# Layer 0 of a two-layer graph network: where a tile's projection and its two groups of transposes stand, and in which order its pieces are read out

## The chip, the cores and the metric

The kernel runs on one core of a Trainium2 chip. TensorE (PE) multiplies matrices and writes them to PSUM, which is divided into eight banks of 512 fp32 numbers a partition. ScalarE (ACT) and VectorE (DVE) read PSUM and the on-chip memory; GpSimd (POOL) works on the on-chip memory in this kernel; SyncE (SP) issues most of the loads. The metric is the device time of one execution in microseconds (us). Times are compared as medians of several runs; traces and profiles come from one profiled execution.

## The reference

A batch of 8 graphs shares one adjacency matrix `adj` (2048 x 2048, rows scaled to sum 1); each of the 2048 nodes has 64 features. Two layers are applied. Cut to what is computed:

```
x, adj: (8, 2048, 64), (2048, 2048)
# layer 0: three supports I, A, 2 A A - I; weights made per node from a 16-wide embedding
w   = einsum('nd,dkio->nkio', embedding, weight0)        # d = 16, k = 3, i = o = 64
b   = einsum('nd,do->no', embedding, bias0)
xg  = [x, A x, (2 A A - I) x]
out = einsum('bnki,nkio->bno', xg, w) + b
x   = layernorm(x + out)
# layer 1: [x, A x, (2 A A - I) x] twice over, times one weight (320 x 64), + bias1
x   = layernorm(x + out1)
```

Layer 0 costs most in the product with 16 weight matrices a support, which are then summed with the node's own 16 embedding numbers.

## The kernel before, in words

The kernel works in four stages. The first hop (A x, to 123 us) and the second hop (A A x, to 226 us) are large products with the adjacency matrix. Layer 0's own products run from 226 to 521 us, and layer 1 from there to the end.

**Layer 0** works on 16 tiles of 128 nodes, in the loop at the end of `pattern` (lines 897 to 939). For a tile three operands are prepared, the tile's features (`of_x`, from a load `xt`), their first hop (`of_hop`) and their second hop (`of_second`). Operand k is kept as three fp32r parts, high, low and a mixture, made by `parts` in three steps: a cast on ScalarE (L327, `hl`), a subtraction on VectorE (L329, `parts`), and a combination, which is one VectorE instruction where `quick` is set (L332), else one of ScalarE (L334) and one of GpSimd (L335). The first hop must be transposed first: eight TensorE transposes of 64 x 64 blocks (`transposed`, L315) into a PSUM tile `pt` of two banks.

`mix0` then runs eight **pieces**, one for each quarter u of the batch and half h of the 16 weight matrices. A piece's product (L423) is 18 matmuls of 64 rows x 512 columns into a PSUM tile `pm` of two banks; two such matmuls use the two halves of TensorE's rows, so they stand as nine pairs. A piece is read out in one of three ways:

- kind "D": one VectorE instruction multiplies the product by the embedding numbers into a tile `aside` (L439), and a VectorE reduction over the eight matrices follows later ("reduce", L468);
- kind "R": eight ScalarE instructions scale the product (L452), and the same VectorE reduction follows;
- kind "P": eight ScalarE instructions scale it, and GpSimd sums ("sum", three instructions of L457, then "add", L461).

GpSimd adds the reduced parts to the tile's sum ("add_reduced", L472). The tile is then scaled to unit variance in four steps spread over the next tile (`scaled_to_unit`: n1 = squares on ScalarE, L368; n2 = a VectorE sum, L379; root on ScalarE, L382; n3 = VectorE's reciprocal, L384, and six GpSimd instructions, L385 to L390).

A tile t whose features are finished is transposed in turn (`transpose`: eight more transposes of L315 into another `pt`, then a ScalarE copy to `hT`, L321), and `project` multiplies it with layer 1's weights (L493, eight fp32 matmuls of 192 columns into two PSUM tiles `pu`); six ScalarE copies (L502) bring the results back. That happens while the next tile is in work.

**What sets the order.** Every instruction of ScalarE, VectorE and GpSimd in this stage goes through `ordered`, which keeps each engine's instructions in the order in which the program writes them. TensorE's instructions and the loads' places follow from that order and from what is ready, as the framework lists them. What is written between which pieces stands in the lists `at[0]` to `at[8]`: `at[n]` is written before piece n, so behind piece n - 1. PSUM tiles come from one pool of four pairs of banks (`bank`), handed out in turn: a new tile waits until the readers of the tile four places earlier are done. Operands' parts, `aside` tiles, `hT` and `sums` come from small pools handed out likewise.

In before, a tile t from 1 to 14 has this order on TensorE: the first product, the hop's transposes for tile t + 1, products two to seven, the feature transposes of tile t - 1, the eighth product, the projection of tile t - 1. The last tile has an order of its own, in which layer 1's first operands (`early`) are prepared as well.

Of the kernel before, what the change touches and what calls it, by code (L numbers as in the profile page):

```python
# [9 lines left out]
F32 = mybir.dt.float32  # L10
# [8 lines left out]
P = 128  # L19
B, N, C = 8, 2048, 64  # L20
NT = N // P
D = 16
# [19 lines left out]
def pattern(  # L42
# [22 lines left out]
    nc = tc.nc  # L65

    def pool(stack, name, bufs, **kw):
        return stack.enter_context(tc.tile_pool(name=name, bufs=bufs, **kw))
# [3 lines left out]
    xcpool = pool(ctx, "fxc", 4)  # L72
# [13 lines left out]
    def bank(name):  # L86

        return psum.tile([P, 2, 512], F32, tag="ps", name=name)
# [9 lines left out]
    def bc(s, t):  # L98
        return z[s][t].rearrange("p (b c) -> p b c", c=C)
# [8 lines left out]
    root = work.tile([P, B], F32, tag="ln_s", name="root")[:, :1]  # L108
    part = keep.tile([P, B], F32, tag="part", name="part")
# [19 lines left out]
    def ordered(ins):  # L129
        if in_order:  # L130
            tc.keep_in_program_order(ins)
# [47 lines left out]
    def weights():  # L179

        vec = nc.vector

        w24 = const.tile([P, C], F32, tag="w24", name="w24")
        yield vec.tensor_add(w24, wl[:, 2, :], wl[:, 4, :])
        yield vec.tensor_sub(v[:, 0, :], wl[:, 0, :], w24)
        for h in range(2):
            q = slice(h * C, (h + 1) * C)
            yield vec.tensor_add(v[q, 0, :], v[q, 0, :], ident[q, q])
        yield vec.tensor_add(v[:, 1, :], wl[:, 1, :], wl[:, 3, :])
        yield vec.tensor_scalar_mul(v[:, 2, :], w24, 2.0)  # L190


        mean = means[:, :4]
        yield vec.tensor_reduce(mean[:, :3], v, AX.X, ALU.add)
        yield vec.tensor_reduce(mean[:, 3:], bias1, AX.X, ALU.add)
        yield vec.tensor_scalar_mul(mean, mean, 1.0 / C)
        yield vec.tensor_tensor(v, v, mean[:, :3].unsqueeze(2).to_broadcast([P, 3, C]), ALU.subtract)
        yield vec.tensor_tensor(bias1, bias1, mean[:, 3:].to_broadcast([P, C]), ALU.subtract)
# [10 lines left out]
    def weight_parts():  # L209
        vec = nc.vector  # L210
        yield vec.tensor_sub(w[0], w[0], w[2])
        yield vec.tensor_scalar_mul(w[2], w[2], 2.0)
        yield from centre(w[0], 8)
        yield from centre(w[2], 8 + 2 * D)
        for k in (0, 2, 1):
            if k == 1:
                yield from centre(w[k], 8 + D)
                yield vec.tensor_scalar_mul(emb_sb, emb_sb, 1.0 - 1.0 / SPLIT)
            yield nc.scalar.copy(w_high[k], w[k])
            yield vec.tensor_tensor(w_low[k], w[k], w_high[k], ALU.subtract)  # L220
            yield vec.scalar_tensor_tensor(w[k], w_low[k], SPLIT, w_high[k], ALU.mult, ALU.add)
            yield vec.tensor_scalar_mul(w_mixed[k], w[k], SPLIT / (SPLIT - 1.0))
            yield vec.tensor_scalar_mul(w_low[k], w_low[k], -SPLIT)
# [82 lines left out]
    def by_half(tt):  # L306
        return tt.rearrange("p j (h n) -> p h j n", h=2)

    def transposed(src, pt=None):

        pt = bank("pt") if pt is None else pt
        for j in range(B // 2):
            for h in range(2):
                q = slice(h * C, (h + 1) * C)
                nc.tensor.transpose(pt[:, h, j * C : (j + 1) * C], src[q, 2 * j * C : 2 * (j + 1) * C], ident[q, q])  # L315
        return pt[:, :, : B // 2 * C].rearrange("p h (j n) -> p h j n", n=C)

    def transpose(src, tag, pt=None):

        tt = xcpool.tile([P, B // 2, P], F32, tag="ln_xc", name=tag)  # L320
        ordered(nc.scalar.copy(by_half(tt), transposed(src, pt)))  # L321
        return tt

    def parts(src, to, view, quick=False):

# [80 lines left out]
    def begin_sum(t):  # L406
        ordered(nc.gpsimd.tensor_tensor(bc(0, t), bc(0, t), ebias[:, t : t + 1, :].to_broadcast([P, B, C]), ALU.add))
# [77 lines left out]
    def project(t, hT, pus=None):  # L485


        for g in range(2):
            pm = bank("pu") if pus is None else pus[g]
            for i in range(2):  # L490
                for j in range(2):
                    q = slice(j * C, (j + 1) * C)
                    nc.tensor.matmul(  # L493
                        pm[:, j, i * 3 * C : (i + 1) * 3 * C], lhsT=hT[q, 2 * g + i, :], rhs=v[q],
                        start=True, stop=True,
                    )
            got = pm[:, :, : 6 * C].rearrange("p j (i k c) -> p j i k c", i=2, k=3)

            order = ["p (i j) c -> p j i c", "p (j i) c -> p j i c", "p (j i) c -> p j i c"]
            to = [bc(k, t)[:, 4 * g : 4 * g + 4, :].rearrange(order[k], j=2) for k in range(3)]  # L500
            for k in range(3):
                ordered(nc.scalar.copy(to[k], got[:, :, :, 2 - k, :]))  # L502
# [249 lines left out]
    pieces = chain(weights(), weight_parts())  # L752
# [74 lines left out]
    last_h = {}  # L827
    sums3 = []

    def last_transposed():  # L830
        last_h["T"] = transpose(h, "hT", sums3[1][0])

    def last_projected():
        project(NT - 1, last_h["T"], (sums3[1][1], sums3[1][0]))
# [46 lines left out]
    def early(i, *kinds):  # L881

        got = third_got.setdefault(i, {})
        for lead, part in sorted(third[i], key=lambda part: -part[0]):
            if part.__name__ in kinds:
                part(got)
        third[i] = [part for part in third[i] if part[1].__name__ not in kinds]

    def go(it):
        return lambda: next(it)  # L890

    s = ("load_sum", "operands")
    h, norm = None, None
    tt = first_tile[0]
    coming = operands(1)
    everything = range(B // 2)
    for t in range(NT):
        got, last = {}, t == NT - 1
        at = [[] for _ in range(9)]
        n1, n2, root, n3 = [lambda: next(norm)] * 4 if t else [nothing] * 4  # L900

        if not last:
            following, of_x, of_hop, of_second = coming
            of_hop = of_hop()
            at[1] += [go(of_x)] * (1 if t else 3)
            at[1] += [n1, lambda: begin_sum(t + 1)]
            if t + 2 < NT:
                at[1] += [lambda: times_r(t + 2)]
            at[1] += [go(of_hop)]
            at[2] += [("reduce", 0, 1), n2, go(of_hop), go(of_hop), ("reduce", 2, 0)]  # L910
            at[3] += [root]
            at[4] += [n3, go(of_second), ("reduce", 3, 0)]
            if t + 2 < NT:
                at[4] += [lambda: got.update(coming=operands(t + 2))]
            at[5] += [("reduce", 1, 1), go(of_second), go(of_second), ("add_reduced", 0, (2, 3))]
            at[7] += [("reduce", 2, 1), ("sum", 0)]
            at[7] += [lambda: got.update(hT=transpose(h, "hT"))] if t else []
            at[8] += [("add", 0, (0, 1)), ("reduce", 3, 1), ("add_reduced", 1, everything)]
            pieces = [(2, 0, "R"), (0, 1, "D"), (3, 0, "R"), (0, 0, "P"), (1, 1, "D"), (1, 0, "P"), (2, 1, "D"), (3, 1, "D")]
        else:  # L920
            at[1] += [n1, n2, root]
            at[2] += [n3, lambda: early(0, "y_high", *s), lambda: early(1, "load_sum")]
            at[3] += [("reduce", 0, 1), ("sum", 0), lambda: early(0, "y_low")]
            at[4] += [lambda: early(1, "y_high", "operands")]
            at[5] += [("reduce", 1, 1), ("reduce", 2, 0), lambda: early(1, "y_low"), ("add", 0, (0, 1))]
            at[6] += [lambda: got.update(hT=transpose(h, "hT")), lambda: early(2, "y_high")]
            at[7] += [("reduce", 2, 1), ("reduce", 3, 0), ("add_reduced", 0, (2, 3)), lambda: early(3, "y_high")]
            at[8] += [("reduce", 3, 1), ("add_reduced", 1, everything), lambda: early(2, "y_low"), lambda: early(3, "y_low")]
            pieces = [(0, 0, "P"), (1, 0, "P"), (0, 1, "D"), (2, 0, "R"), (1, 1, "D"), (3, 0, "R"), (2, 1, "D"), (3, 1, "D")]
        norm_now = mix0(t, tt, at, pieces)  # L930
        if t:
            project(t - 1, got["hT"])
        if "coming" in got:
            coming = got["coming"]
            next(coming[1])
            next(coming[1])
        norm, h = norm_now, z[0][t]
        if not last:
            tt = following
# [481 lines left out]
```

## Time and profile before

| What | Value |
|---|---|
| Time, median of 3 runs (lowest to highest) | 757.3 us (756.75 to 757.43) |
| The profiled execution's own time, and its span in the trace | 756.74 us, 755.0 us |
| Busy over the span: PE, DVE, ACT, POOL | 744.3, 618.1, 453.4, 277.9 us |
| Layer 0, 226.5 to 521 us (294.5): PE, DVE, ACT, POOL | 293.1, 271.7, 218.6, 208.7 us |
| Two tiles in the middle, 283.5 to 320.2 us (36.7): PE, DVE, ACT, POOL | 36.7, 34.1, 27.6, 27.6 us |
| Granted TensorE clock, share of full speed | 0.997 |

How to read it: "busy" is the time in which an engine has an instruction under way. Matmuls overlap and their ends are modelled, so what counts on TensorE is the time from one start to the next, and whether a row says that it was idle and for whom it waited. The chain that ended last is followed back from the last instruction; an engine with a high share of that chain sets the time. A row of a timeline gives start, length, engine, line, operation, output <- input, and in brackets the idle time ahead of it with the instruction that ended it.

### The profile page before, as it was taken

How to read it: one execution, taken by the hardware profiler on the slowest of the kernel's cores; microseconds unless marked ns; L12 is line 12 of the kernel's file. 1: busy time of each engine (PE TensorE's matmuls, PEld its weight loads, DVE VectorE, ACT ScalarE, POOL GpSimd, SP SyncE). 2: the span in 40 equal slices, each digit the busy share in tenths (PEclk: the TensorE clock that was granted, in tenths of full speed). 3: DMA queues.
4: the chain of work that ended last, by engine and by line, in shares of the span. 5: the costliest groups of instructions: out<-in, count | busy, mean ns of one | idle time of the engine just before them, and what ended most of it. 6: DMA issues, size and time to landing. Idle time of an engine off the chain costs nothing.

```text
span 755.0 us, 13518 instructions
## 1 busy us (share of the span) xinstructions
PE 744.3 (99%) x4942; PEld 613.0 (81%) x4942; DVE 618.1 (82%) x965; ACT 453.4 (60%) x1106; POOL 277.9 (37%) x299
## 2 busy tenths in 40 slices
PE   9999999999999999999999999999999999999995
PEld 6887888888888788888888888887788888888885
DVE  6768888999978999999999999979588557778563
ACT  5437444878755777777777777778877662112111
POOL 0001111133253877777777777664000000021430
PEclk9999999999999999999999999999999999999998
DMA  9998987555420000000000000004454454665621
GB/s 322 376 400 282 326 279 278 175 160 168 153 85 15 16 16 16 15 15 17 20 24 15 16 15 1 2 30 127 128 165 142 137 171 138 180 183 167 205 88 47
DMA packets 73691, 96.49 MB, mean 128 GB/s; under 512 B 5009, under 2 KB 48529, under 8 KB 73489
## 3 DMA queue, kind: packets, MB, share of 16 engines
q1 hardware_dynamic: 62208, 76.66, 32.2%
q10 hardware_dynamic: 11408, 18.89, 6.8%
q8 instruction: 41, 0.67, 0.4%
q14 instruction: 34, 0.27, 0.1%
HBM read 76.65 MB, written 18.87 MB: 127 GB/s over the span
## 4 chain that ended last, share of the span: by engine, by line
PE 92%; DVE 5%; issue 1%; POOL 1%; ACT 0%; DVEq 0%; POOLq 0%
PE pm L423 29%; PE accT L697 27%; PE acc L269 15%; PE a L269 10%; PE accT L269 6%; PE pu L493 2%; DVE aside L439 2%; DVE sums L468 1%; PE pt L315 1%; DVE parts L332 1%; PE first L145 1%; PE accT L853 1%; DVE parts L329 1%; ACT aside L452 0%; PE accT L493 0%
## 5 line engine op out<-in xcount | busy, mean ns | idle before, releaser
L697 PE MATMUL accT<-s,hl 128*128 128x512 f32 x896 | 206.1, 391 | 0.4 <-DVE aside L439 0.4
L697 PEld LDWEIGHTS accT<-s,hl 128*128 128x128 f32 x896 | 167.4, 188 | 36.7 <-DVE aside L439 0.9
L452 ACT ACTIVATE aside<-pm,pack_sb 128x128 f32<-128x128 f32 x512 | 140.2, 402 | 40.2 <-PE pm L423 40.2
L423 PE MATMUL pm<-wh,hl 64*128 64x512 f32 x768 | 154.6, 399 | 0.7 <-DVE aside L439 0.7
L423 PE MATMUL pm<-wm,parts 64*128 64x512 f32 x768 | 150.1, 388 | 0.0
L423 PE MATMUL pm<-wl,parts 64*128 64x512 f32 x768 | 149.7, 387 | 0.0
L684 ACT CAST s<-raw 128x1024 fp32r<-128x1024 bf16 x104 | 110.1, 1059 | 37.0 <-ACT hl L249 27.6
L468 DVE TENSOR_REDUCE sums<-aside 128x128 f32<-128x1024 f32 x96 | 115.9, 1210 | 3.2
L269 PE MATMUL acc<-hl,s 128*128 128x512 f32 x512 | 116.9, 390 | 0.0
L269 PEld LDWEIGHTS acc<-hl,s 128*128 128x128 f32 x512 | 95.9, 188 | 20.8 <-DVE z L578 0.9
L249 ACT CAST hl<-z 128x256 fp32r<-128x256 f32 (+1 forms) x96 | 47.8, 516 | 62.8 <-PE acc L269 21.6
L439 DVE TENSOR_TENSOR aside<-pm,pack_sb 128x1024 f32<-128x1024 f32 x64 | 78.3, 1223 | 8.7 <-PE pm L423 6.3
L423 PEld LDWEIGHTS pm<-wm,parts 64*128 64x128 f32 x768 | 71.9, 184 | 15.7
L423 PEld LDWEIGHTS pm<-wh,hl 64*128 64x128 f32 x768 | 72.3, 185 | 15.0 <-DVE aside L439 1.0
L457 POOL TENSOR_TENSOR aside<-aside 128x1024 f32<-128x1024 f32 (+2 forms) x48 | 71.6, 1491 | 32.3 <-ACT aside L452 29.8
L423 PEld LDWEIGHTS pm<-wl,parts 64*128 64x128 f32 x768 | 72.1, 185 | 13.8
L269 PE MATMUL a<-hl,s 128*128 128x512 f32 (+1 forms) x352 | 73.4, 370 | 0.0
L253 DVE TENSOR_TENSOR hl<-z,hl 128x512 fp32r<-128x512 f32 (+1 forms) x96 | 57.8, 610 | 16.6 <-ACT hl L249 7.6
L269 PEld LDWEIGHTS a<-hl,s 128*128 128x128 f32 x352 | 61.9, 188 | 11.3
L403 POOL TENSOR_TENSOR s<-s,part 128x8 f32<-128x8 f32 x16 | 7.0, 440 | 166.9 <-DVE s L402 145.8
L302 POOL TENSOR_TENSOR z<-z,got 128x512 f32<-128x512 f32 x3 | 4.8, 1622 | 144.1 <-ACT got L301 144.1
L368 ACT ACTIVATE sq<-z 128x512 f32<-128x512 f32 x31 | 20.0, 651 | 48.8 <-DVE z L304 46.6
(138 smaller groups left out, 948.4 us busy)
## 6 DMA issues: line engine op xcount, KB each, us to landing
raw<-in_adj SPq DMA_DIRECT2D x58, 512.0 KB, 6.0
raw<-sums_of SPq DMA_DIRECT2D x64, 256.0 KB, 2.9
sums_of<-z ACTq DMA_DIRECT2D x16, 512.0 KB, 6.8
raw<-quarters SPq DMA_DIRECT2D x32, 256.0 KB, 2.7
raw<-in_adj SPq DMA_DIRECT2D x16, 384.0 KB, 3.5
quarters<-seen ACTq DMA_DIRECT2D x16, 256.0 KB, 5.9
xt<-in_xT SPq DMA_DIRECT2D x16, 256.0 KB, 2.7
z<-in_x SPq DMA_DIRECT2D x15, 256.0 KB, 6.7
```

The source lines that it names most:

```text
L249: ordered(nc.scalar.copy(to[0], src))
L253: ordered(nc.vector.tensor_tensor(to[1], src, to[0], ALU.subtract))
L269: nc.tensor.matmul(accs[i], lhsT=s[:, i * P : (i + 1) * P], rhs=hl[h], start=(first and h == 0), stop=(last and h == 1),)
L368: ordered(nc.scalar.activation(sq, src, AF.Square))
L423: nc.tensor.matmul(pm[:, j], lhsT=tt[k][n][q, u, :], rhs=w_parts[n][k][q, ds, :], start=(k == 0 and n == 0), stop=(k == 2 and n == 2),)
L439: ordered(nc.vector.tensor_tensor(side_by_side(a), got, e, ALU.mult))
L452: ordered(nc.scalar.activation(to[d], got, AF.Copy, scale=emb_sb[:, t, h * DD + d : h * DD + d + 1]))
L457: ordered(nc.gpsimd.tensor_tensor(to, to, more, ALU.add))
L468: ordered(nc.vector.tensor_reduce(to, src, AX.X, ALU.add))
L493: nc.tensor.matmul(pm[:, j, i * 3 * C : (i + 1) * 3 * C], lhsT=hT[q, 2 * g + i, :], rhs=v[q], start=True, stop=True,)
L684: ordered(nc.scalar.copy(s, got["raw"]))
L697: nc.tensor.matmul(acc[i][:, c], lhsT=hl[h][:, i * P : (i + 1) * P], rhs=S[:, c * 512 : (c + 1) * 512], start=(kk == 0 and h == 0), stop=( ...
```

## The change

The change touches only layer 0's loop and splits `transpose` in two, so that the ScalarE copy (`keep_transposed`) can be written apart from the transposes.

- For tiles 0 to 14 the hop's transposes for the next tile but one, and the feature transposes of the tile before, are written between two tiles, behind the projection, and go into the two halves of one PSUM tile `pt` (columns 0 to 255 and 256 to 511 of each of its two banks). ScalarE's cast of the hop half is written there too. The copy of the feature half (`hT`) is written behind the next tile's first piece.
- So a projection comes one tile later: behind tile t stands the projection of tile t - 2. The last tile takes the projection that is left behind its second piece, and its own feature transposes and projection as before.
- The pieces of tiles 0 to 14 go R, D, P, D, P, D, R, D instead of R, D, R, P, D, P, D, D.
- The third operand's steps start one place earlier, and GpSimd's "sum" and "add" stand in `at[6]` behind them; the reductions and additions of the quarter 3 move to the end of the tile. In the last tile, the preparation of layer 1's third operand moves ahead of the two last reductions.

```diff
-    def transpose(src, tag, pt=None):
-
-        tt = xcpool.tile([P, B // 2, P], F32, tag="ln_xc", name=tag)
-        ordered(nc.scalar.copy(by_half(tt), transposed(src, pt)))
+    def keep_transposed(got):
+        tt = xcpool.tile([P, B // 2, P], F32, tag="ln_xc", name="hT")
+        ordered(nc.scalar.copy(by_half(tt), got))
         return tt
+
+    def transpose(src, pt=None):
+        return keep_transposed(transposed(src, pt))
...
+        if t > 1:
+            at[1] += [lambda: hT.append(keep_transposed(hT.pop()))]
         if not last:
             following, of_x, of_hop, of_second = coming
-            of_hop = of_hop()
-            at[1] += [go(of_x)] * (1 if t else 3)
-            at[1] += [n1, lambda: begin_sum(t + 1)]
+            if t == 0:
+                of_hop = of_hop()
+                at[1] += [go(of_hop), go(of_x), go(of_x)]
+            at[1] += [go(of_hop), go(of_x), n1, lambda: begin_sum(t + 1)]
             if t + 2 < NT:
                 at[1] += [lambda: times_r(t + 2)]
-            at[1] += [go(of_hop)]
-            at[2] += [("reduce", 0, 1), n2, go(of_hop), go(of_hop), ("reduce", 2, 0)]
-            at[3] += [root]
-            at[4] += [n3, go(of_second), ("reduce", 3, 0)]
+            at[2] += [("reduce", 0, 1), go(of_hop), n2, ("reduce", 2, 0)]
+            at[3] += [root, go(of_second)]
+            at[4] += [n3, ("reduce", 1, 1), go(of_second), go(of_second)]
             if t + 2 < NT:
                 at[4] += [lambda: got.update(coming=operands(t + 2))]
-            at[5] += [("reduce", 1, 1), go(of_second), go(of_second), ("add_reduced", 0, (2, 3))]
-            at[7] += [("reduce", 2, 1), ("sum", 0)]
-            at[7] += [lambda: got.update(hT=transpose(h, "hT"))] if t else []
-            at[8] += [("add", 0, (0, 1)), ("reduce", 3, 1), ("add_reduced", 1, everything)]
-            pieces = [(2, 0, "R"), (0, 1, "D"), (3, 0, "R"), (0, 0, "P"), (1, 1, "D"), (1, 0, "P"), (2, 1, "D"), (3, 1, "D")]
+            at[6] += [("reduce", 2, 1), ("sum", 0), ("add", 0, (0, 1))]
+            at[8] += [("reduce", 3, 0), ("reduce", 3, 1), ("add_reduced", 0, (2, 3)), ("add_reduced", 1, everything)]
+            pieces = [(2, 0, "R"), (0, 1, "D"), (0, 0, "P"), (1, 1, "D"), (1, 0, "P"), (2, 1, "D"), (3, 0, "R"), (3, 1, "D")]
         else:
             at[1] += [n1, n2, root]
-            at[2] += [n3, lambda: early(0, "y_high", *s), lambda: early(1, "load_sum")]
+            at[2] += [lambda: project(t - 2, hT.pop()), n3, lambda: early(0, "y_high", *s), lambda: early(1, "load_sum")]
...
-            at[6] += [lambda: got.update(hT=transpose(h, "hT")), lambda: early(2, "y_high")]
-            at[7] += [("reduce", 2, 1), ("reduce", 3, 0), ("add_reduced", 0, (2, 3)), lambda: early(3, "y_high")]
-            at[8] += [("reduce", 3, 1), ("add_reduced", 1, everything), lambda: early(2, "y_low"), lambda: early(3, "y_low")]
+            at[6] += [lambda: hT.append(transpose(h)), lambda: early(2, "y_high")]
+            at[7] += [("reduce", 2, 1), lambda: early(3, "y_high")]
+            at[8] += [
+                lambda: early(2, "y_low"), ("reduce", 3, 0), ("add_reduced", 0, (2, 3)),
+                ("reduce", 3, 1), ("add_reduced", 1, everything), lambda: early(3, "y_low"),
+            ]
...
         norm_now = mix0(t, tt, at, pieces)
-        if t:
-            project(t - 1, got["hT"])
-        if "coming" in got:
-            coming = got["coming"]
-            next(coming[1])
-            next(coming[1])
+        if last:
+            project(t - 1, hT.pop())
+        else:
+
+            if hT:
+                project(t - 2, hT.pop())
+            pt = bank("pt")
+            if "coming" in got:
+                coming = [*got["coming"]]
+                coming[2] = coming[2](pt[:, :, : N // 8])
+                for part in (coming[1], coming[2], coming[1]):
+                    next(part)
+            if t:
+                hT.append(transposed(h, pt[:, :, N // 8 :]))
```

More of the change, by code (lines that the diff above doesn't have):

```diff
@@ L830, in last_transposed @@
     def last_transposed():
-        last_h["T"] = transpose(h, "hT", sums3[1][0])
+        last_h["T"] = transpose(h, sums3[1][0])
     def last_projected():
@@ L895, in pattern @@
     coming = operands(1)
-    everything = range(B // 2)
+    everything, hT = range(B // 2), []
     for t in range(NT):
```

## The prediction

> **What bounds the kernel now.** I read the chain that ended last first, because it says which engine a shorter or longer layer 0 would move; then TensorE's rows in order of time, for the price of each break; then ScalarE's and VectorE's rows, for what becomes ready when. From the page, and from the chain in order of time (start, length, what):
>
> ```profile
> span 755.0 us, 13518 instructions
> PE 92%; DVE 5%; issue 1%; POOL 1%; ACT 0%; DVEq 0%; POOLq 0%
> ```
>
> ```profile
> 301.91 0.24 PE pt L315 x8
> 302.15 12.33 PE pm L423 x108
> 314.48 0.25 PE pt L315 x8
> 314.73 2.12 PE pm L423 x18
> 316.85 1.30 PE pu L493 x16
> 318.15 2.06 PE pm L423 x18
> 320.22 0.25 PE pt L315 x8
> ```
>
> TensorE is the whole chain. A tile of layer 0 takes 18.33 us (projections start at 280.03 and 500.03, twelve tiles apart), of which 72 pairs of matmuls at 0.227 are 16.3; the rest is three breaks. TensorE's rows price them:
>
> ```profile
> 301.75 0.40 PE L315 MATMUL pt<-ident,z 64*128 64x64 f32 x8
> 301.96 0.48 PE L423 MATMUL pm<-wh,hl 64*128 64x512 f32 x2
> 302.28 0.39 PE L423 MATMUL pm<-wl,parts 64*128 64x512 f32 x2
> 302.51 0.39 PE L423 MATMUL pm<-wm,parts 64*128 64x512 f32 x2
> ...
> 316.46 0.39 PE L423 MATMUL pm<-wm,parts 64*128 64x512 f32 x2
> 316.69 1.46 PE L493 MATMUL pu<-v,hT 64*128 64x192 f32 x16
> 317.86 0.53 PE L423 MATMUL pm<-wh,hl 64*128 64x512 f32 x2
> 318.22 0.40 PE L423 MATMUL pm<-wl,parts 64*128 64x512 f32 x2
> ```
>
> Eight transposes cost 0.21 and a projection 1.17, start to next start. The first pair after a break takes 0.32 to 0.36 instead of 0.23. So all that putting the three breaks together can save is two restarts, some 0.2 us a tile. Between 266 and 520 no row of TensorE waits for anybody: there is nothing else to win there, and much that could start to wait.
>
> **The change, part by part** (line numbers of before; those behind L315 move by 2 in the changed file).
>
> *The transposes do not come together.* In the built order of the changed kernel, from tile 2 to 13, the projection and the eight hop transposes stand between two tiles, but the eight feature transposes stand inside the next tile's first product, behind 7 of its 18 matmuls, between the two halves of one pair. The build makes them wait for ScalarE's cast of the hop half (hl<-pt, L327), since both halves now lie in one tile of two banks. Before, the two groups had a bank pair each and the feature transposes waited for nothing late. When is that cast done? ScalarE now has to copy the projection out first, then cast the next x, then the hop. Its rows:
>
> ```profile
> 317.61 1.76 ACT L502 COPY z<-pu 128x256 f32<-128x256 f32 x6 [2.25 <-PE pu L493]
> 319.20 0.67 ACT L327 CAST hl<-xt 128x512 fp32r<-128x512 f32 x1
> ```
>
> ```profile
> 230.86 0.67 ACT L327 CAST hl<-xt 128x512 fp32r<-128x512 f32 x1
> 231.37 0.65 ACT L327 CAST hl<-pt 128x512 fp32r<-128x512 f32 x1
> ```
>
> Counted from the projection's start (316.69): copies begin at +0.92 (they wait for its first half), the x cast 1.59 later, the hop cast 0.51 later, and it lasts 0.65: +3.67. TensorE restarts 0.05 after what it waits for (a VectorE row ends at 520.97, TensorE starts at 521.02): **+3.72**. When could TensorE take the transposes? 1.17 + 0.21 is +1.38. Then the next tile's first product needs its bank pair. Four pairs go round; in between lie two for the projection and one for the transposes, so it is that of the last product, which VectorE must have read. The last product's matmuls end 0.16 after the projection's start, VectorE's read lasts 1.23: +1.5 at the earliest, +2.5 if VectorE is behind (below). Seven matmuls take 0.33 + 3 x 0.23 = 1.0. So TensorE is ready at +2.5 to +3.5 and waits 0.2 to 1.2 us, every time until +3.72.
>
> Behind the wait: 0.21 of transposes, 0.10 restart, and 137 matmuls. Their halves are now out of step (row half 1 has 69 left, half 0 has 68), so 69 slots at 0.227, 15.66. Sum 3.72 + 0.21 + 0.10 + 15.66 = **19.7 us a tile instead of 18.33, +1.37**. The wait itself is shown by no row of before. From below it costs nothing (cast early enough): 1.17 + 0.42 + the bank wait 0.1 + one restart 0.1 + 16.3 = 18.1; from above VectorE decides (20.4, next). I take 19.7, since every term of it has a row.
>
> *A rule to weigh.* No row of before has two engines at one bank pair at once. "PSUM — Partial Sum Buffer" of the Trainium skill, section "Terms", says that two engines at the same bank and quadrant at once is a collision error, reads against reads included; by that the two groups cannot overlap however the list is ordered, and the sum stands. If halves of a bank were independent, the transposes could go at once and a tile would take some 18.4.
>
> *VectorE.* Its read of the hop half (L329, 0.68) now waits for ScalarE's copy of the features, which stands behind the next tile's first piece: product's end 1.84 behind the transposes, 2.02 of evictions, 0.59 of copy. Everything else of VectorE's tile is queued behind that read. From there to its last product's read is, by start-to-start spacings of its rows, 0.72 + 0.61 (L329, L332), 4 x 1.23 (L439), 4 x 1.13 (L468), 0.59 (L379), 0.11, 0.72 + 0.61: 12.8. Closing the ring: 1.84 + 2.65 + 12.8 + 0.05 + 1.0 = 18.4, under 19.7, so it is not the bound; its last read ends about +2.5. But L332 can lose to GpSimd:
>
> ```profile
> 258.31 4.90 POOL L457 TENSOR_TENSOR aside<-aside 128x1024 f32<-128x1024 f32 x3 [0.69 <-ACT aside L452]
> 258.38 2.88 DVE L332 SCALAR_TENSOR_TENSOR parts<-hl,parts 128x512 fp32r<-128x512 f32 x1
> ```
>
> That took 2.88 instead of 0.69; beside GpSimd's shorter sums it takes 1.67 (302.39). One such loss a tile gives 19.4, two 20.4.
>
> *The third operand ahead of GpSimd's sum* removes the 2.88 of tile 1 and nothing in the later tiles, where its L332 already takes 0.69 (331.88). *Pieces in turn*: cost nothing either way, for the four bank pairs cover two ScalarE pieces in a row today (324.69 to 329, TensorE never waits). The load of the next x keeps its step and its place on SP's queue; no DMA is added or moved past another. Begin of the sum and the scaling by r stay in GpSimd's order.
>
> *Start.* Before, the second projection starts at 280.03. After: tile 0 ends at 243.25 as now; 0.21 hop transposes, 0.1, 16.4 of tile 1: 260.0; the first product of tile 2 starts at 260.2, seven matmuls to 261.2; the hop cast, behind no copies yet, ends at 261.36; then 0.21 + 0.10 + 15.66: 277.3. That is where the first projection starts, a tile later than now: **-2.7**, being the projection (1.3) that now goes to the last tile, and VectorE's waits of tile 1 and 2 (0.72 and 0.25, with restarts).
>
> *End.* Tile 15 takes the projection that is left (1.3) between its second and third product. It waits for a feature copy behind ScalarE's first piece (0.59 + 2.02 + the product: 0.9 of wait), and the fourth product for an eviction behind that (0.3). Its first product starts 2.5 behind the last projection instead of 1.17 (1.3). **+3.8**. Layer 1's wait of 0.41 at 521.02 and its restart go, as VectorE has one reduce less before its last read: -0.65.
>
> *Sum*: -2.7 + 12 x 1.37 + 3.8 - 0.65 = **+16.8**. The profiled execution took 756.74 (1.74 around its span of 755.0), 0.56 under the median of 757.3. So 773.5.
>
> **Rivals.**
> 1. *The cast gates (above)*: 773.5, with tiles of 19.45 to 20.0: 770 to 777. For it: the wait is in the built program and every length has a row.
> 2. *VectorE becomes the bound* through two losses to GpSimd a tile, 20.4: 12 x 0.7 more, 782. For it: the 2.88 row. Against: GpSimd's long sum now comes later.
> 3. *A cheaper gate*: the split pair costs no slot (0.23) and VectorE is early, or the cast comes 0.4 earlier: tiles of 19.1: 766.
> 4. *Faster*: the wait is covered. If the cast is done by +2.5, before TensorE has done its seven matmuls, tiles take 18.1: 12 x -0.23, -2.7, -0.65, and +2.5 at the end: 753. It decides at a cast end of +2.5; ScalarE's six copies alone end at +2.68, which speaks against it.
> 5. *It cancels out*: tiles of 18.4 and the dearer last tile: 758.
>
> **How the numbers follow.** Chances: 0.72, 0.10, 0.12, 0.04, 0.02. Range 765 to 780: rival 1 whole, rival 3, the near part of rival 2. A difference under 0.2% (1.5 us) can hardly be told from none here: faster 0.04, same 0.02, slower 0.94.
>
> **What would show it.** Right: twelve waits of TensorE ahead of the feature transposes (L315) released by ScalarE's hl cast; projections 19.7 apart; VectorE idle until ScalarE's feature copy; the waits at 262 and 521 gone. Wrong: projections 18.1 to 18.4 apart, or a TensorE that waits for VectorE longer than for ScalarE.

## The result and the profile after

The changed kernel takes 775.58 us (median; 775.49 to 775.81), the kernel before 757.02 beside it (756.62 to 757.43): ratio 1.0246, 95% interval [1.0228, 1.0263]. The profiled execution's span is 773.7 us, 18.7 more than before's 755.0. The granted clock is 0.998 (before: 0.997).

The page of the changed kernel, in the order in which before was read: span, shares of the chain that ended last, and the group of first matmuls (its last columns: idle time of TensorE ahead of it, and for whom).

```profile
span 773.7 us, 13482 instructions
...
PE 62%; DVE 17%; POOL 7%; ACT 7%; issue 6%; DVEq 0%; POOLq 0%
...
L425 PE MATMUL pm<-wh,hl 64*128 64x512 f32 x768 | 223.8, 394 | 9.8 <-DVE aside L441 9.8
```

TensorE had 92% of the chain and has 62%; in layer 0 the chain now runs through VectorE, ScalarE and GpSimd. TensorE has no more to do than before, so its rows around one gap between tiles tell what it stands for (start, length, and in brackets the idle time with the one that ended it):

```profile
338.53 0.32 PE L495 MATMUL pu<-v,hT 64*128 64x192 f32 x1
338.55 0.39 PE L425 MATMUL pm<-wm,parts 64*128 64x512 f32 x1
338.69 1.38 PE L495 MATMUL pu<-v,hT 64*128 64x192 f32 x14
339.62 1.75 ACT L504 COPY z<-pu 128x256 f32<-128x256 f32 x6 [0.51 <-PE pu L495]
...
341.02 0.50 PE L425 MATMUL pm<-wh,hl 64*128 64x512 f32 x2 [0.55 <-DVE aside L441]
341.20 0.68 ACT L329 CAST hl<-xt 128x512 fp32r<-128x512 f32 x1
...
341.73 0.64 ACT L329 CAST hl<-pt 128x512 fp32r<-128x512 f32 x1
...
341.83 0.39 PE L425 MATMUL pm<-wh,hl 64*128 64x512 f32 x1
...
342.47 0.46 PE L315 MATMUL pt<-ident,z 64*128 64x64 f32 x8 [0.26 <-issue]
342.71 0.47 PE L425 MATMUL pm<-wl,parts 64*128 64x512 f32 x1
342.75 0.47 PE L425 MATMUL pm<-wh,hl 64*128 64x512 f32 x1
```

There are two waits in a gap. The next tile's product starts at 341.02, when VectorE has read the product four pairs back (the forecast's "+2.5": it is +2.49). Seven matmuls later TensorE stops until 342.47, 0.10 after ScalarE's cast of the hop half has ended (341.73 + 0.64 = 342.37). The trace lists this second wait under "issue" or under a GpSimd instruction, but it ends 0.09 to 0.14 behind the end of the cast in all eleven gaps from 302 to 501; in kernel 2 below, where the same wait is longer, the list names the cast itself four times. Projections start at 279.03 and 516.35, twelve tiles apart: **19.78 us a tile**, where it was 18.33. (The first of the twelve takes 20.18: there TensorE waits 1.42 for VectorE, at 282.43, and the cast has long ended.)

VectorE's waits in the changed kernel (total, times, longest), and its chain in time through the middle of a tile (start, length, what):

```profile
DVE parts L331 <- ACT hT L320: 39.4, 12, 3.4
```

```profile
344.47 2.18 ACT aside L454 x8
346.65 0.48 ACT hT L320
347.12 0.02 issue
347.15 0.69 DVE parts L331
347.84 0.60 DVE parts L334
```

Twelve times VectorE stands 3.3 us until ScalarE has copied the features, behind the next tile's first piece. The wait is new, and the chain runs through it.

### The profile page after: what moved, and what is told of

It reads as the page before. It is cut to its first block, busy times and chain, and to the rows that moved or that the text cites. A ratio compares the mean times of both kernels' runs of the same rounds, so it can differ in the third digit from the quotient of the medians.

```text
span 773.7 us, 13482 instructions
## 1 busy us (share of the span) xinstructions
PE 751.4 (97%) x4942; PEld 642.1 (83%) x4942; DVE 607.0 (78%) x965; ACT 453.1 (59%) x1106; POOL 285.4 (37%) x299
## 4 chain that ended last, share of the span: by engine, by line
PE 62%; DVE 17%; POOL 7%; ACT 7%; issue 6%; DVEq 0%; POOLq 0%
PE accT L699 27%; PE acc L269 15%; PE a L269 9%; DVE sums L470 6%; DVE aside L441 6%; PE accT L269 6%; POOL aside L459 5%; ACT aside L454 4%; PE pm L425 3%; DVE parts L334 2%; DVE parts L331 2%; ACT hl L329 2%; POOL z L392 1%; ACT hT L320 1%; PE first L145 1%
## 5 line engine op out<-in xcount | busy, mean ns | idle before, releaser
L425 PE MATMUL pm<-wh,hl 64*128 64x512 f32 x768 | 223.8, 394 | 9.8 <-DVE aside L441 9.8
L425 PE MATMUL pm<-wl,parts 64*128 64x512 f32 x768 | 219.9, 388 | 0.0
L425 PE MATMUL pm<-wm,parts 64*128 64x512 f32 x768 | 219.2, 387 | 0.0
L425 PEld LDWEIGHTS pm<-wh,hl 64*128 64x128 f32 x768 | 120.7, 184 | 18.9 <-DVE aside L441 11.8
L425 PEld LDWEIGHTS pm<-wm,parts 64*128 64x128 f32 x768 | 120.5, 184 | 6.7
L425 PEld LDWEIGHTS pm<-wl,parts 64*128 64x128 f32 x768 | 120.1, 184 | 5.8
L459 POOL TENSOR_TENSOR aside<-aside 128x1024 f32<-128x1024 f32 (+2 forms) x48 | 77.6, 1617 | 7.0 <-ACT aside L454 4.5
L253 DVE TENSOR_TENSOR hl<-z,hl 128x512 fp32r<-128x512 f32 (+1 forms) x96 | 56.0, 591 | 16.0 <-ACT hl L249 7.2
```

The costliest lines, as they stand in the source:

```text
L253: ordered(nc.vector.tensor_tensor(to[1], src, to[0], ALU.subtract))
L425: nc.tensor.matmul(pm[:, j], lhsT=tt[k][n][q, u, :], rhs=w_parts[n][k][q, ds, :], start=(k == 0 and n == 0), stop=(k == 2 and n == 2),)
L459: ordered(nc.gpsimd.tensor_tensor(to, to, more, ALU.add))
```

## The experiments

All times are medians, with the kernel before timed on the same chip (756.9 to 757.1). A gate is a wait that every tile has to pass; a ring is the work from one such wait to the same wait of the next tile, and the longest ring sets the time of a tile. Theory A: the cast alone gates the tile. Theory B: VectorE's ring (its late read of the hop half and all that is queued behind it) lies close behind the cast and holds the tile once the cast does not. Theory C: the order of the pieces and additions uses VectorE up.

**1. Feature transposes ahead of the hop's cast.**

```diff
+            if t:
+                hT.append(transposed(h, pt[:, :, N // 8 :]))
             if "coming" in got:
...
-            if t:
-                hT.append(transposed(h, pt[:, :, N // 8 :]))
```

> The changed kernel, but the feature transposes are written ahead of the hop transposes and ScalarE's cast of the hop half; then TensorE does not wait for the cast, and the built order has projection and both groups together. The ScalarE copy of the features stays behind the next tile's first piece. Theory A (the cast alone sets the 19.8 us of a tile): the tile falls to 18.2 to 18.3 and the time to 757, twelve times 1.5 less. Theory B (VectorE's ring, held by its read of the hop half behind the feature copy, lies close behind): in the changed kernel it closes from one last read to the next in 19.7 us, of which 1.1 are the wait, the transposes and the broken pair in the first product; without them 18.6, so 12 x 1.2 less: 761. Theory C (neither; the new order of pieces and additions costs the time): 775.

Measured: 769.03, ratio 1.0155 [1.0138, 1.0171]; tiles of 19.33. All three numbers missed, A's by 12 us, B's by 8, C's by 6. TensorE's gap in this kernel:

```profile
337.19 1.46 PE L495 MATMUL pu<-v,hT 64*128 64x192 f32 x16
...
338.49 0.66 PE L315 MATMUL pt<-ident,z 64*128 64x64 f32 x16
...
340.06 0.49 PE L425 MATMUL pm<-wh,hl 64*128 64x512 f32 x2 [0.91 <-DVE aside L441]
```

The sixteen transposes stand together and no matmul waits for a cast; TensorE waits 0.9 a tile for VectorE instead. So A alone falls; whether C does, kernel 3 tells. VectorE's ring here is 19.3, not the forecast 18.4, and its two L334 of a tile show why: they took 1.26 and 1.42 beside GpSimd, where the forecast had an undisturbed one (0.69 long) for both. From the hop half's read (345.18) to the end of the last product's read (359.32) it takes 14.14, forecast 12.8; the two L334 are 1.30 of that.

**2. The copy of hT ahead of the first piece (the cast's gate stays).**

```diff
-            at[1] += [lambda: hT.append(keep_transposed(hT.pop()))]
+            at[0] += [lambda: hT.append(keep_transposed(hT.pop()))]
```

> The changed kernel, but the ScalarE copy of the features is written ahead of the next tile's first piece instead of behind it, so that VectorE's read of the hop half can come some 2 us earlier; the feature transposes still wait for the cast. Theory A: VectorE's waits go (39 us of idle time ahead of that read fall under 15), TensorE's waits of 0.55 for VectorE go, its waits for the cast grow by the same: time as the changed kernel, 775 within 1.5. Theory B in its strong form (VectorE's ring sets the time): 765 to 770. Theory C: 775, but with VectorE late as before.

Measured: 775.11, ratio 1.0243 [1.0226, 1.026]; tiles of 19.72, as theory A had it (VectorE's idle time ahead of that read falls from 39.4 to 6.1). TensorE's wait moves whole from VectorE to the cast:

```profile
341.59 0.46 PE L315 MATMUL pt<-ident,z 64*128 64x64 f32 x8 [1.03 <-POOL z L474]
...
361.36 0.46 PE L315 MATMUL pt<-ident,z 64*128 64x64 f32 x8 [1.07 <-ACT hl L329]
```

The cast ends at 341.49 and at 361.22, so it is the same wait under two names.

**3. Both edits.**

> Both edits: features transposed first, and copied ahead of the first piece. Theories A and B alike: neither wait is left; a tile is 1.17 of projection, 0.42 of transposes, one restart, and 16.3 of products, 18.1 to 18.2, and the time 755, with 754 to 757 as bounds. Theory C: 770 or more, since order of pieces and of the additions stays.

Measured: 756.07, ratio 0.9987 [0.9978, 0.9997], inside the bounds of A and B; tiles of 18.19 from 297 on. Its gap:

```profile
333.95 1.46 PE L495 MATMUL pu<-v,hT 64*128 64x192 f32 x16
...
335.25 0.66 PE L315 MATMUL pt<-ident,z 64*128 64x64 f32 x16
...
335.72 0.47 PE L425 MATMUL pm<-wh,hl 64*128 64x512 f32 x2
336.03 0.39 PE L425 MATMUL pm<-wl,parts 64*128 64x512 f32 x2
```

From 297 on no wait is left between tiles. The new order of the pieces is all in here, so C falls. The four kernels make a square: with both gates 775.6, without the cast's 769.0, without the copy's 775.1, with neither 756.1. Taking away one leaves the other ring, of 19.72 or 19.33, in charge.

**4. Hop cast ahead of the x cast.**

```diff
-                for part in (coming[1], coming[2], coming[1]):
+                for part in (coming[2], coming[1], coming[1]):
```

> The changed kernel, but ScalarE casts the hop half ahead of the x tile, so the cast ends 0.5 earlier; the built order then has the feature transposes behind 6 matmuls of the first product instead of 7, so no pair is split. Theory A: a tile is shorter by 0.5 of cast and 0.1 to 0.2 of a split pair, as far as TensorE is ready by then (it is 0.26 after its last product of the seven): 12 x 0.4 to 0.7 less, 767 to 771. Theory B: VectorE's ring shrinks by the same wait and pair: the same range; its own share shows in TensorE's wait for VectorE, which stays at 0.5 or grows. Theory C: 775.

Measured: 771.42, ratio 1.0189 [1.0172, 1.0206], just above the range of both theories; tiles of 19.45. The cast and the transposes of one gap:

```profile
339.57 0.66 ACT L329 CAST hl<-pt 128x512 fp32r<-128x512 f32 x1
...
339.96 0.39 PE L425 MATMUL pm<-wm,parts 64*128 64x512 f32 x1
340.33 0.46 PE L315 MATMUL pt<-ident,z 64*128 64x64 f32 x8
```

From the projection's start (336.86) the cast ends at +3.37 instead of +3.84. The list shows no wait of TensorE for it, but the transposes still start 0.09 to 0.15 behind its end in every gap from 281 on: the cast still gates. The transposes stand behind five matmuls, not six, so a pair is split here too, and two more matmuls come behind the wait than in the changed kernel: 3.47 + 15.99 (340.33 to 356.32) is 19.46. TensorE's wait of 0.55 for VectorE stays, and VectorE's ring has next to nothing to spare: ahead of the transposes TensorE is idle for only some 0.14 (from 339.96 and one matmul of 0.23 to 340.33).

**5. Feature transposes in banks of their own.**

```diff
-                hT.append(transposed(h, pt[:, :, N // 8 :]))
+                hT.append(transposed(h))
```

> The changed kernel, but the feature transposes get a bank pair of their own again; the projection and both groups still stand together between two tiles, and the copy of hT stays behind the first piece. If sharing one bank pair is what ties the cast and the copies to the transposes (the theory), TensorE does projection and both groups in one go (1.17 + 0.42), waits only for the bank pair of the first product (ScalarE's copies of the projection's first half, 0.5 to 1 us at most, and less if they are early), and VectorE's read of the hop half no longer waits for the copy of hT: tiles of 18.2 to 18.5, 757 to 761. If the position between the tiles is what costs, whatever the banks, it stays at 769 to 776.

Measured: 758.6, ratio 1.0023 [1.0014, 1.0032], inside the theory's range; tiles of 18.31, no wait of TensorE listed between tiles from 269 on. One gap:

```profile
336.17 1.22 DVE L441 TENSOR_TENSOR aside<-pm,pack_sb 128x1024 f32<-128x1024 f32 x1 [1.21 <-PE pm L425]
...
337.27 0.69 PE L315 MATMUL pt<-ident,z 64*128 64x64 f32 x16
337.81 0.50 PE L425 MATMUL pm<-wh,hl 64*128 64x512 f32 x2
...
340.17 0.68 DVE L331 TENSOR_TENSOR parts<-pt,hl 128x512 fp32r<-128x512 f32 x1
```

With the place of the work unchanged and the copy still late, both gates go. What makes them is the sharing of one bank pair: TensorE's write of one half then waits for ScalarE's read of the other, and VectorE's read for ScalarE's copy. (One more pair is used a tile, so the first product also gets another pair than in the changed kernel. That is not what frees it: VectorE's last read ends at 337.39 here, ahead of 337.81.) The first tiles still lose 1.76 and 1.10, and the last tile is still the dearer one.

**6. The order of the pieces alone, on the kernel before** (its transposes and projection untouched).

```diff
-            pieces = [(2, 0, "R"), (0, 1, "D"), (3, 0, "R"), (0, 0, "P"), (1, 1, "D"), (1, 0, "P"), (2, 1, "D"), (3, 1, "D")]
+            pieces = [(2, 0, "R"), (0, 1, "D"), (0, 0, "P"), (1, 1, "D"), (1, 0, "P"), (2, 1, "D"), (3, 0, "R"), (3, 1, "D")]
```

(with the lists `at[3]` to `at[8]` of the change)

> The kernel before with only the new order of the pieces, of the reductions and additions, and the third operand ahead of GpSimd's sum; projection and transposes stand as before. Theory (the order costs nothing where the transposes do not wait): 756 to 758, tiles of 18.3; the 0.72 wait of tile 1 behind the 2.88 us subtraction goes, and a wait of 1.5 to 2 in tile 0 takes its place, because GpSimd's sum of tile 0 now starts beside VectorE's first subtraction. Rival (the order itself uses VectorE up): over 760.

Measured: 764.65, ratio 1.0103 [1.0088, 1.0119]; tiles of 18.98. The theory's number is missed and the rival's is met, but not by its mechanism, for VectorE holds nobody up between the later tiles (the wait of 1.5 to 2 expected in tile 0 did not come either; 0.41 at 251.66 and 0.64 at 259.12 did). TensorE's waits and one gap of this kernel show

```profile
PE pu L493 <- ACT hT L321: 4.7, 13, 0.4
```

```profile
315.65 2.18 ACT L452 ACTIVATE aside<-pm,pack_sb 128x128 f32<-128x128 f32 x8 [1.91 <-PE pm L423]
...
317.66 0.64 ACT L321 COPY hT<-pt 128x512 f32<-128x512 f32 x1
...
317.59 0.39 PE L423 MATMUL pm<-wm,parts 64*128 64x512 f32 x2
318.35 1.57 PE L493 MATMUL pu<-v,hT 64*128 64x192 f32 x16 [0.37 <-ACT hT L321]
319.62 0.53 PE L423 MATMUL pm<-wh,hl 64*128 64x512 f32 x2
```

In before, the copy of hT stands behind a "D" piece, when ScalarE is free; in the new order the last piece but one is an "R", and the copy queues behind its eight evictions. Every projection waits 0.37 for it. From start to start that wait costs more: the projection comes 0.76 behind the last pair (in before 0.23) and the next product 1.27 behind the projection (in before 1.17), together 0.63 of the 0.65 a tile.

**7. The same, with that one pair of pieces exchanged.**

```diff
-            at[6] += [("reduce", 2, 1), ("sum", 0), ("add", 0, (0, 1))]
+            at[6] += [("sum", 0), ("add", 0, (0, 1))]
+            at[7] += [("reduce", 2, 1)]
...
-            pieces = [(2, 0, "R"), (0, 1, "D"), (0, 0, "P"), (1, 1, "D"), (1, 0, "P"), (2, 1, "D"), (3, 0, "R"), (3, 1, "D")]
+            pieces = [(2, 0, "R"), (0, 1, "D"), (0, 0, "P"), (1, 1, "D"), (1, 0, "P"), (3, 0, "R"), (2, 1, "D"), (3, 1, "D")]
```

> The kernel before with the new order of pieces, which took 764.65 with tiles of 18.98 and a wait of 0.37 of each projection for the copy of hT, but with the pieces (3, 0, R) and (2, 1, D) exchanged, so that the copy of hT again stands behind a piece of VectorE's and not behind eight ScalarE evictions. If that place of the copy is what the order cost: tiles of 18.33, 756 to 758. If the order of the reductions and additions is: 762 to 765.

Measured: 756.02, ratio 0.9991 [0.9981, 1.0]; tiles of 18.33, as before and as the first of the two expectations had it. The place of the copy was the whole cost (the reduction of the piece exchanged goes with it). Beside the kernel before the difference is too small to be told.

**8. GpSimd's losses in VectorE's ring, taken away in part.** Kernel 1 without two GpSimd instructions a tile, the scaling by 1/deviation and the product with r, so its output is not scaled:

```diff
-        ordered(nc.gpsimd.tensor_tensor(src, src, wide(r), ALU.mult))
         yield
...
-            if t + 2 < NT:
-                at[1] += [lambda: times_r(t + 2)]
```

> The kernel with the feature transposes ahead of the hop's, which took 769.03, with two of GpSimd's instructions of each tile left out: the product of the operand two tiles on with r (L750) and that of the features with 1/deviation (L392), so the output is not scaled. VectorE's two subtractions of a tile lay beside them and took 1.26 and 1.42 instead of 0.69. If VectorE's ring binds there and those losses are what the forecast of 18.4 for this ring missed, tiles go from 19.33 to 18.1 to 18.5: 754 to 759. If the ring is held by the wait for the copy of hT itself and the losses lie in its slack: 766 to 769.

Measured: 783.22, ratio 1.0354 [1.0338, 1.037]; tiles of 20.09. Less work made it 14 us slower than kernel 1, which neither expectation had; the twelve tiles are some 10 of it. VectorE and GpSimd in this kernel:

```profile
337.55 5.41 POOL L458 TENSOR_TENSOR aside<-aside 128x1024 f32<-128x1024 f32 x3
...
338.24 2.77 DVE L334 SCALAR_TENSOR_TENSOR parts<-hl,parts 128x512 fp32r<-128x512 f32 x1
```

The scaling by 1/deviation (1.43 long) had stood between this L334 and GpSimd's sum. Without it the sum starts earlier and L334 meets its longest instruction. The ring's arithmetic holds: 19.33, less 0.57 for the first L334 (1.26 to 0.69, now that the product with r is gone from beside it), more 1.35 for the second (1.42 to 2.77), is 20.11, against 20.09.

**9. The same without the two large instructions of the sum** (its output lacks their terms as well).

```diff
-            for to, more in ((one, other), (one[:, :2], one[:, 2:]), (one[:, 0], one[:, 1])):
+            for to, more in ((one[:, 0], one[:, 1]),):
```

> The kernel of 783.22 (feature transposes first, without GpSimd's products by r and by 1/deviation) with two of the three instructions of each GpSimd sum (L459) left out as well, the two large ones, so the output lacks terms too. In that kernel VectorE's subtraction L334 began 0.7 behind the sum and took 2.77, tiles of 20.09. Theory (VectorE's ring binds and each loss beside GpSimd counts in full): L334 falls to 0.69, the ring from 20.09 to 18.0, and TensorE's own work of 18.2 becomes the bound: 754 to 757. Rival (the wait for the copy of hT holds the ring, whatever GpSimd does): 766 or more.

Measured: 757.57, ratio 1.0011 [1.0002, 1.0021]; tiles of 18.42. The theory's 754 to 757 is missed by 0.6, because L334 still meets the sum's last instruction:

```profile
347.52 1.11 DVE L334 SCALAR_TENSOR_TENSOR parts<-hl,parts 128x512 fp32r<-128x512 f32 x1
```

19.33 - 0.57 - 0.73 + 0.42 = 18.45, against 18.42. So in kernel 1 VectorE's ring was the bound, and every loss to GpSimd counted in full, though the wait for the copy of hT (2.3) stood in the same ring all the time.

**10. Both gates off, and the old order in tile 0 alone.** Kernel 3 with before's pieces and lists in the first tile:

```diff
+            if t:
...
+                pieces = [(2, 0, "R"), (0, 1, "D"), (0, 0, "P"), (1, 1, "D"), (1, 0, "P"), (2, 1, "D"), (3, 0, "R"), (3, 1, "D")]
+            else:
...
+                pieces = [(2, 0, "R"), (0, 1, "D"), (3, 0, "R"), (0, 0, "P"), (1, 1, "D"), (1, 0, "P"), (2, 1, "D"), (3, 1, "D")]
```

> The changed kernel with both gates off (feature transposes first, copy of hT ahead of the first piece), and in tile 0 alone the old order of pieces and additions. That kernel without the last step took 756.07 and had two waits of TensorE for VectorE left, 1.74 at 244.8 and 0.94 at 281.1. If both come from GpSimd's early sum in tile 0, they go: 753.4 (753 to 754). If only the first does: 754.3. If VectorE loses as much to GpSimd a tile later, as before's 2.88 us subtraction did: 755.5 to 756.5.

Measured: 754.25, ratio 0.996 [0.9946, 0.9974]: faster than before, the only one of these that can be told from it on that side by over 0.2%. The time is the one expected if only the first wait goes, but the rows show otherwise: in the traces layer 0, from its first product to layer 1's first long product, takes 291.0 us here (227.12 to 518.12) and 293.65 in kernel 3 (225.88 to 519.53), and the 1.74 and the 0.94 are gone but for 0.25 at 279.71. Layer 0 began 1.24 later in this profile, which the edit does not explain. Why the first wait stood there, the changed kernel's own rows show:

```profile
239.08 5.22 POOL L459 TENSOR_TENSOR aside<-aside 128x1024 f32<-128x1024 f32 x3 [4.49 <-ACT aside L454]
239.25 2.77 DVE L331 TENSOR_TENSOR parts<-z,hl 128x512 fp32r<-128x512 f32 x1
242.05 1.66 DVE L334 SCALAR_TENSOR_TENSOR parts<-hl,parts 128x512 fp32r<-128x512 f32 x1
243.64 1.21 DVE L441 TENSOR_TENSOR aside<-pm,pack_sb 128x1024 f32<-128x1024 f32 x1
...
244.90 0.50 PE L425 MATMUL pm<-wh,hl 64*128 64x512 f32 x2 [1.74 <-DVE aside L441]
```

In tile 0 GpSimd has nothing to normalise, so its sum starts as soon as the two "P" pieces are there, which the new order brings earlier: 0.17 ahead of VectorE's subtraction, which takes 2.77 instead of 0.68.

## Why the prediction was right, point by point

The time came out 2.1 us above the forecast, and rival 1, which the forecast stood on, is what happened.

- *The transposes do not come together; the cast gates.* Right. Forecast and measured, from the projection's start: copies +0.92 and +1.09, end of the cast +3.67 and +3.84, restart +3.72 and +3.94. Behind the wait 15.97 were forecast; 342.47 to the next projection at 358.24 is 15.77. Tile 19.7 and 19.78. So the slot that the split pair costs is not lost where the forecast put it, among the 137 matmuls: the projection's first matmul runs beside the last one of the product. It comes back at the copies, which start +1.09 behind the projection where a pair is split and +0.86 in kernels 1, 3 and 5. The odd slot is in the rows: 337.85 and 337.87, 338.08 and 338.10, single matmuls of the two halves, one slot apart, until the projection puts itself between them at 338.53.
- *VectorE's ring, "18.4, not the bound".* The size failed. The stretch from the hop half's read to the last product's read was put at 12.8; in the changed kernel it is 13.55 (347.15 to 360.70), 0.73 of it the L334 that takes 1.42 beside GpSimd's scaling. Alone the ring holds the tile at 19.33 (kernel 1, where the other L334 loses 0.57 too), not 18.4; in the changed kernel all that it has to spare is TensorE's second wait, 0.26 to 0.32 in ten of the gaps. So the two rings lay 0.3 to 0.4 apart, not 1.3, and the statement that the cast gates was half of the truth: undoing it alone gains 6.6 us of 19.5. Rival 2's mechanism (losses to GpSimd) was there, but with one loss of 0.73 a tile, where it needed two of 1.0.
- *Its own signs.* Three came: no wait at 521, tiles of 19.7, VectorE idle until the copy of the features. Two came in part: at 262 the 0.72 for VectorE is gone, but 0.36 at 262.80 (the cast) and 1.74 at 244.90 are new, and the waits for the cast are not listed under it. One sign of being wrong came true: TensorE waits longer for VectorE than for the cast (0.53 to 0.55 in a gap against 0.26 to 0.32). It was a bad sign, for a wait ahead of a later gate costs nothing; kernel 2 takes the wait for VectorE away, and the tile stays at 19.72.
- *Pieces in turn and the third operand early cost nothing.* Right for this change from tile 2 on (kernel 3: tiles of 18.19; in the first tiles the new order costs some 1.8 us, kernel 10), but not for the reason given. Alone they cost 7.5 us (kernel 6), through a queue that the forecast did not look at: what else ScalarE has to do behind that piece.
- *All that the joined breaks can save, some 0.2 us a tile.* Measured where nothing gates: 18.33 - 18.19 = 0.14.
- *Start, -2.7.* Mis-sized: -0.49 (from layer 0's first product at 225.94 to the projection at 279.03 is 53.09; before's second stood at 53.58). The forecast took it that VectorE's waits of the first tiles go; 1.74 at 244.90 came instead, through the earlier sum of tile 0, with its restart. (The 1.42 at 282.43 lies behind the projection, in the twelve tiles.) So the start is 2.2 dearer than forecast, the largest error of the sum.
- *End +3.8, and layer 1's wait -0.65.* Measured +3.98 (516.35 to 538.30 is 21.95, and was 17.97; the wait of 0.75 for the copy of hT is in it) and -0.72 (from the projection to layer 1's transposes 12.50, and was 13.22).
- *Sum.* -0.49 + 12 x 1.44 (17.3) + 3.98 - 0.72 = +20.1; layer 0 began 0.51 earlier and the last store's tail was 0.88 shorter, neither of which the change explains: +18.7. So the terms were 3.3 short of what they measured, and 1.4 of that was made good by luck.

"PSUM — Partial Sum Buffer" of the Trainium skill, section "Terms", the rule that was weighed, is what these runs agree with in the order that the build gives: kernel 5 differs from the changed one only in the banks, and the waits are gone. The waits are put in by the build; no run here let two engines into the shared pair at once, so the collision itself is shown by none.

"SBUF — State Buffer" of the Trainium skill, section "Who interferes with whom", says that a VectorE instruction with two SBUF inputs contends with a GpSimd instruction that reads SBUF, for a shared pair of ports that is an exclusive lock, and that VectorE's reductions never contend. The rows agree: L331 and L334 take 2.77 instead of 0.68 and 0.69 beside the sum (in tile 0 the sum's first instruction runs from 239.08 to 241.47, and L331, begun at 239.25, ends at 242.02), and the reduction at 338.42 in the changed kernel, beside the sum of 336.67, takes 1.22 as everywhere.

## What to carry to other kernels

Two users put into one bank pair are tied to each other's readers: before packing them, list who writes and who reads each half, in the order of every engine's queue, and see whether a late reader now stands ahead of an early writer. Where two rings lie close, undoing one gains a part at most; only the square of both edits tells what each is worth. A ring's length is to be summed from rows that stand beside the same neighbours as after the change: the same VectorE step (L334) took 0.69, 1.11, 1.26, 1.42 or 2.77 here.

## What the runs showed of the hardware that was not expected

- Taking work from GpSimd can make VectorE slower: without two GpSimd instructions a tile grew from 19.33 to 20.09, because one of them, 1.43 long, had kept a VectorE instruction apart from a longer one of GpSimd.
- The two row halves of TensorE keep running one slot apart when a group is put between the two matmuls of a pair, through all 137 matmuls that follow, and come together only in the next gap. The 137 take no longer for it; the copies behind the projection that follows start one slot later (+1.09 instead of +0.86).
